# Moving the x loads, the bias additions and the key copies in the hand-written end of an attention stage

## The chip, the core and the metric

The kernel runs on one core of one Trainium2 chip. The metric is the device time in microseconds (us). Engines are named as in the profile: PE is TensorE, DVE is VectorE, ACT is ScalarE, POOL is GpSimd, SP is SyncE, which here only issues DMAs.

## The reference, cut to what matters

The computation has two layers, both with a residual. The first is cross-attention of 3200 tokens (32 batches of 100, 512 features) on a context of 722 rows, with a causal mask, so that only the first 100 context rows of a batch count. The second is a feed-forward layer with 16 routed experts and a shared one.

```python
def xattn(Q, K, V, WQ, WK, WV, Wfc, bfc):            # 16 heads of 32
    q, k, v = heads(Q @ WQ.T), heads(K @ WK.T), heads(V @ WV.T)
    scores = einsum('bhqd,bhkd->bhqk', q, k) / sqrt(32)
    attn = softmax(where(tril(ones(Sq, Skv)), scores, -inf))
    y = einsum('bhqk,bhkd->bhqd', attn, v)
    return y.transpose(0, 2, 1, 3).reshape(B, Sq, 512) @ Wfc.T + bfc

def ffn(h):
    # each expert takes its 12 best tokens of each batch by softmax(h @ gate_w.T):
    # cap = int(100 * 2.0 / 16)
    out = scatter_add((gelu(x_tok @ Wg[e].T) * (x_tok @ Wu[e].T)) @ Wd[e].T * topk_w)
    return out + (gelu(h @ Ws_g.T) * (h @ Ws_u.T)) @ Ws_d.T

x = x + xattn(layernorm(x), ctx, ctx, ...)
x = x + ffn(layernorm(x))
```

## The kernel before, in words

Every projection splits its float32 operands into a high and a low part and makes three matmul passes into one PSUM bank (`mm3`, L56).

**Units.** Attention is cut into 32 units u = 4 * sb + c: a super-block sb of four batches (400 tokens) and a chunk c of four heads. A unit consists of these steps, each a small function:

- `kload` (L210) loads the keys of the unit from DRAM into kt; `vload` (L215) loads the values v of a super-block.
- `qproj`/`qkeep`: q = normed x times WQ on PE into a "kv" PSUM buffer, copied to SBUF by ACT (L230).
- `scores`: 16 small matmuls into sc (L240).
- `sm_max` (DVE, L251, eight per half, two halves hb), `sm_sub` (POOL, L260), `sm_exp` (ACT, L264), `sm_sum` (DVE, L269 and L270), `sm_mul` (POOL, L275): the softmax.
- `turns`/`keeps` (`p_turn` on PE, L281; `p_keep` on ACT, L286): the probabilities transposed, one pair of batches at a time, and copied to pt.
- `values`: pt times v (L296). `y_keep`: split by ACT (L101) and DVE (L102), written to DRAM (yD, L306).

The keys and values themselves are projected on the way, block j and chunk ck at a time: `kproj` puts keys into a kv buffer, `kkeep` copies them to kk on ACT (L204) and writes them to kD on SP (L205); `vproj`/`vkeep` do the same for values in three of four iterations. In the iteration with ck = 3 (`vv` is false) there is no value projection.

**The loop.** The units run as a software pipeline. Iteration u (u from 0 to 28) projects q of unit u, does the softmax of unit u - 1, turns and values of unit u - 2, and y of unit u - 3. The kernel is under a manual schedule: every engine runs its instructions in the order in which the program states them, and SP issues its DMAs in that order into one queue. DMA completion uses eight semaphores in turn, so that each issue on SP also waits for the DMA eight before it. PSUM has two kv buffers and two ms buffers (turns, values).

**The end.** Units 29, 30 and 31 are written out by hand in `last_units`. Between their steps stand those of the feed-forward layer's first group of three 128-row tiles, the object `pr`. `pr.load_y` loads the attention output (yh, yl, L1003). For tile i, `pr.load_x(i)` loads x (L1011), `pr.bias(i)` adds bfc to it on POOL (L1014), `pr.fc(i)` is y times Wfc on PE into a kv buffer (L56), `pr.add(i)` adds the two on DVE (L1023), `pr.stats(i)` (DVE, L1029, L1030), `pr.rsqrt(i)` (POOL, L1036, L1037) and `pr.norm(i)` (DVE, L1044) are the layer norm, and `pr.turn(i)` transposes the tile on PE (L955), after which ACT and DVE make the parts xh and xl (L956, L957). `F.chunk_load` loads a chunk of expert weights (wraw, L705), `F.chunk_cast` and `F.chunk_low` split it on ACT (L713) and POOL. `F.begin` starts the feed-forward matmuls (gate-up "gu", then down "dn"), which fill the rest of the kernel.

The order around the change, in the code before:

```python
            u = NU - 3
            scores(u - 1)
            y_keep(u - 3)
            kload(u)
            vload(nsb - 1)
            for i in range(pr.nt):
                pr.load_x(i)
            F.chunk_load()
            kload(u + 1)
```

Of the kernel before, what the change touches and what calls it, by code (L numbers as in the profile page):

```python
# [60 lines left out]
def attention(tc, K, F):  # L61
    nc = tc.nc
    with ExitStack() as ctx, ExitStack() as kvctx:
# [34 lines left out]
        nsb = K.nsb  # L98
# [114 lines left out]
        def vload(sb):  # L213
            v = vp.tile([S, 4, D], F32, name="v")
            nc.sync.dma_start(v, K.vD[sb * SB:(sb + 1) * SB, :].rearrange("(b s) d -> s b d", b=4))  # L215
            for b in range(4):
                cur["v", sb, b] = v[:, b, :]
# [167 lines left out]
        def turns(u, *bs):  # L385
            for b in bs:
                p_turn(u, b)
# [12 lines left out]
        def last_units(pr):  # L400

            gp = nc.gpsimd

            def maxes(u):
                for hb in range(2):
                    sm_max(u, hb)
                    sm_sub(u, hb)

            u = NU - 3
            scores(u - 1)  # L410
            y_keep(u - 3)
            kload(u)
            vload(nsb - 1)
            for i in range(pr.nt):
                pr.load_x(i)
            F.chunk_load()
            kload(u + 1)
            maxes(u - 1)
            qkeep(u, qproj(u))
            turns(u - 2, 0, 1)  # L420
            keeps(u - 2, 0, 1)
            turns(u - 2, 2, 3)
            sm_exp(u - 1, 0)
            keeps(u - 2, 2, 3)
            sm_exp(u - 1, 1)
            for hb in range(2):
                sm_sum(u - 1, hb)
                sm_mul(u - 1, hb)
            pr.fc(0)
            values(u - 2)  # L430

            u = NU - 2
            scores(u - 1)
            y_keep(u - 3)
            F.chunk_load()
            pr.bias(0)
            pr.bias(1)
            maxes(u - 1)
            pr.add(0)
            pr.stats(0)  # L440
            pr.rsqrt(0)
            qkeep(u, qproj(u))
            turns(u - 2, 0, 1)
            sm_exp(u - 1, 0)
            keeps(u - 2, 0, 1)
            sm_exp(u - 1, 1)
            pr.fc(1)
            for hb in range(2):
                sm_sum(u - 1, hb)
                sm_mul(u - 1, hb)  # L450
            turns(u - 2, 2, 3)
            keeps(u - 2, 2, 3)
            F.chunk_cast(0, 0)
            pr.norm(0)
            pr.add(1)
            kload(u + 1)
            values(u - 2)

            u = NU - 1
            scores(u - 1)  # L460
            y_keep(u - 3)
            pr.store(0)
            pr.bias(2)
            pr.stats(1)
            maxes(u - 1)
            pr.rsqrt(1)
            pr.fc(2)
            qkeep(u, qproj(u))
            F.ask(1, lambda: ps_kv.tile([128, D], F32, name="kv"))
            F.preps[1].load_x(0)  # L470
            F.preps[1].load_x(1)
            turns(u - 2, 0, 1)
            sm_exp(u - 1, 0)
            keeps(u - 2, 0, 1)
            pr.add(2)
            sm_sum(u - 1, 0)
            sm_mul(u - 1, 0)
            sm_exp(u - 1, 1)
            pr.norm(1)
            turns(u - 2, 2, 3)  # L480
            keeps(u - 2, 2, 3)
            sm_sum(u - 1, 1)
            sm_mul(u - 1, 1)
            pr.stats(2)
            pr.turn(0)
            values(u - 2)
            pr.turn(1)
            F.chunk_cast(0, 1)
            pr.rsqrt(2)
            pr.store(1)  # L490

            scores(u)
            y_keep(u - 2)
            F.chunk_low(0, 0, gp)
            F.chunk_low(0, 1, gp)
            maxes(u)
            turns(u - 1, 0, 1)
            keeps(u - 1, 0, 1)
            turns(u - 1, 2, 3)
            keeps(u - 1, 2, 3)  # L500
            values(u - 1)
            F.preps[1].fc(0)
            pr.norm(2)
            sm_exp(u, 0)
            sm_sum(u, 0)
            sm_mul(u, 0)
            sm_exp(u, 1)
            pr.turn(2)
            y_keep(u - 1)
            sm_sum(u, 1)  # L510
            sm_mul(u, 1)
            pr.store(2)
            F.chunk_cast(0, 2)
            scctx.close()
            F.open_gu()
            F.begin(pr.done())
            F.chunk_low(0, 2, gp)
            F.preps[1].bias(0)
            F.preps[1].add(0)
            for i in range(3):  # L520
                F.chunk_cast(1, i)
                F.chunk_low(1, i, gp)
            F.preps[1].bias(1)
            turns(u, 0, 1)
            keeps(u, 0, 1)
            pr.logits()
            turns(u, 2, 3)
            keeps(u, 2, 3)
            F.begun()
            values(u)  # L530
            pr.tokens()
            y_keep(u)

        with tc.manual_schedule(engines={mybir.EngineType.Pool}):
            prologue()
            for u in range(NU - 3):
                sb, c = divmod(u, NC4)
                a, back = u - 1, u - 2
                a = a if a >= 0 else None
                back = back if back >= 0 else None  # L540
                j, ck = divmod(u - KS, NC4)
                j += 2
                kv = j in blocks
                vv = kv and ck < KVB[j]
                jn, d = divmod(u + NC4 - KS, NC4)
                jn += 2
                jl, dl = divmod(u + NC4 + 2 - KS, NC4)
                jl += 2
                xs = sb + 1 < nsb
                xn = divmod(u + 5, NC4) if u + 5 < NU else None  # L550
                if u > 0:
                    kload(u)
                if jl in blocks and (jl, dl) != (3, 0):
                    ctx_load(jl, dl)
                sn, bn = divmod(u + 6, NC4)
                if sn < nsb:
                    x_load(sn, bn)
                if FC_AT <= u < FC_AT + NC4:
                    fr = load_w(3, u - FC_AT)
                if u == FC_AT + NC4:  # L560
                    F.load_consts()
                if u == FC_AT + NC4 + 2:
                    F.split_consts()
                if a is not None:
                    scores(a)
                if u - 3 >= 0:
                    y_keep(u - 3)
                if a is not None:
                    sm_max(a, 0)
                    sm_sub(a, 0)  # L570
                    sm_max(a, 1)
                    sm_sub(a, 1)
                qkeep(u, qproj(u))
                if a is not None:
                    sm_exp(a, 0)
                if back is not None:
                    p_turn(back, 0)
                    p_turn(back, 1)
                    p_keep(back, 0)
                    p_keep(back, 1)  # L580
                if xn:
                    x_stats(*xn)
                if a is not None:
                    sm_exp(a, 1)
                    sm_sum(a, 0)
                    sm_mul(a, 0)
                if kv:
                    kkeep(j, ck, kproj(j, ck))
                if c == 1:
                    vload(sb)  # L590
                if back is not None:
                    p_turn(back, 2)
                    p_turn(back, 3)
                    p_keep(back, 2)
                    p_keep(back, 3)
                if a is not None:
                    sm_sum(a, 1)
                    sm_mul(a, 1)
                if xn:
                    x_norm(*xn)  # L600
                if jn in blocks:
                    ctx_split(jn, d)
                if FC_AT <= u < FC_AT + NC4:
                    F.fc_split(u - FC_AT, fr)
                if u == 0:
                    vkeep(1, 1, vproj(1, 1))
                if vv:
                    vkeep(j, ck, vproj(j, ck))
                if xs:
                    x_turn(sb + 1, c, vv)  # L610
                if back is not None:
                    values(back)
            kvctx.close()
            F.open_first()
            pr = F.prep(0, lambda: ps_kv.tile([128, D], F32, name="kv"),
                        lambda: ps_ms.tile([128, NC4, 128], F32, name="ms"))
            pr.load_y()
            last_units(pr)
# [690 lines left out]
```

## Time and profile before

| | us |
|---|---|
| three runs | 1692.14, 1692.4, 1695.08 |
| median | 1692.4 |
| the profiled execution: time | 1691.74 |
| its span in the profile | 1689.5 |
| PE busy | 1665.4 (99%) |
| DVE busy | 921.2 (55%) |
| ACT busy | 679.7 (40%) |
| POOL busy | 624.3 (37%) |

The span runs from the first to the last recorded instruction of the execution. "Busy" is the time in which an engine works on an instruction. The clock that PE is granted is a number between 0 and 1; its mean over this execution is 0.996. A wait is named by the engine that waits, the instruction that waits, and the one whose end released it, as `PE ms L281 <- ACT pt L286`. The profile's durations come from this one execution.

### The profile page before, as it was taken

Reading aid. Unit: us, or ns where it says so; the run is one execution under the profiler, and the core shown is the slowest. Engines: PE = TensorE matmul, PEld = TensorE weight load, DVE = VectorE, ACT = ScalarE, POOL = GpSimd, SP = SyncE. Lnnn points to the kernel's source line nnn. Section 1 sums busy time; section 2 is a strip of 40 time slices with the busy share of each in tenths; the row PEclk is TensorE's granted clock in tenths of the full one; section 3 lists DMA queues with packets and bytes.
Section 4 is the critical chain, followed back from the end, with each engine's and each line's share of the span. In section 5 each row is a group of like instructions: output and inputs, shape, how many; then the busy total and the mean of one; then the engine's idle time right before and its main releaser. Section 6 shows DMA issues by size and latency. Waiting matters only on the chain.

```text
span 1689.5 us, 28055 instructions
## 1 busy us (share of the span) xinstructions
PE 1665.4 (99%) x10854; PEld 1531.3 (91%) x10854; DVE 921.2 (55%) x2208; ACT 679.7 (40%) x1088; POOL 624.3 (37%) x541
## 2 busy tenths in 40 slices
PE   8999999989999999999999999999999999999999
PEld 7998889869989999989899999999999999999998
DVE  4878777655433434344555555555555555555542
ACT  4556555443111111122434444444444444444442
POOL 3877777570111011010243444333344333344011
PEclk9999999989999999999999999999999999999999
DMA  7555544545322214211445554555554455555452
GB/s 219 160 161 181 160 160 152 173 159 183 101 78 98 75 68 139 87 44 42 142 155 159 167 165 143 160 152 151 165 168 144 157 160 151 160 163 157 134 165 63
DMA packets 106741, 237.46 MB, mean 141 GB/s; under 512 B 13777, under 2 KB 58034, under 8 KB 106608
## 3 DMA queue, kind: packets, MB, share of 16 engines
q1 hardware_dynamic: 93248, 209.98, 37.4%
q0 software_dynamic: 12944, 25.22, 7.7%
q8 instruction: 85, 1.39, 0.3%
q10 hardware_dynamic: 416, 0.48, 0.1%
q14 instruction: 48, 0.39, 0.1%
HBM read 181.90 MB, written 53.73 MB: 139 GB/s over the span
## 4 chain that ended last, share of the span: by engine, by line
PE 93%; ACT 2%; DMA 2%; DVE 1%; POOL 1%; issue 1%; SPq 0%; ACTq 0%; POOLq 0%; DVEq 0%
PE gu L56 49%; PE dn L56 24%; PE kv L56 11%; PE m L56 3%; PE ms L281 2%; PE ms L296 2%; PE sc L240 1%; POOL p L260 1%; DMA x<-x 1%; ACT pt L286 1%; DMA kD<-kk 1%; PE m L1078 1%; DVE p L251 1%; PE ms L171 0%; ACT p L264 0%
## 5 line engine op out<-in xcount | busy, mean ns | idle before, releaser
L56 PE MATMUL gu<-xh,whl 128*128 128x384 f32 (+1 forms) x3200 | 643.8, 333 | 0.7 <-ACT xh L956 0.7
L56 PEld LDWEIGHTS gu<-xh,whl 128*128 128x128 f32 x3200 | 558.9, 188 | 17.8 <-ACT xh L956 0.9
L56 PE MATMUL dn<-whl,hh 128*128 128x512 f32 x1168 | 368.0, 396 | 0.0
L730 DVE TENSOR_TENSOR whl<-wraw,whl 128x1536 fp32r<-128x1536 f32 x142 | 249.7, 1758 | 205.7 <-ACT whl L729 205.6
L935 POOL DMA_INDIRECT gx<-xnD,iq x180 | 226.7, 1259 | 362.1 <-DVE big L966 301.9
L56 PE MATMUL gu<-xl,whl 128*128 128x384 f32 (+1 forms) x1600 | 337.2, 332 | 0.0
L56 PEld LDWEIGHTS gu<-xl,whl 128*128 128x128 f32 x1600 | 280.0, 188 | 0.1
L764 ACT CAST hh<-g 128x384 fp32r<-128x384 f32 (+1 forms) x200 | 100.9, 505 | 409.2 <-DVE g L761 409.2
L56 PEld LDWEIGHTS dn<-whl,hh 128*128 128x128 f32 x1168 | 215.8, 188 | 36.9
L761 DVE TENSOR_TENSOR g<-g,gu 128x384 f32<-128x384 f32 (+1 forms) x200 | 108.3, 541 | 247.9 <-PE gu L56 243.3
L729 ACT CAST whl<-wraw 128x1536 fp32r<-128x1536 f32 x142 | 209.7, 1477 | 64.8 <-PE dn L56 61.7
L56 PE MATMUL dn<-whl,hl 128*128 128x512 f32 x584 | 230.6, 395 | 0.0
L760 ACT ACTIVATE g<-gu 128x384 f32<-128x384 f32 (+1 forms) x200 | 96.3, 481 | 239.2 <-PE gu L56 239.1
L765 DVE TENSOR_TENSOR hl<-g,hh 128x384 fp32r<-128x384 f32 (+1 forms) x200 | 111.2, 556 | 114.2 <-ACT hh L764 114.2
L977 POOL DMA_INDIRECT out_dram<-x,isl x48 | 77.7, 1619 | 173.0 <-ACT x L976 163.2
L56 PEld LDWEIGHTS dn<-whl,hl 128*128 128x128 f32 x584 | 109.8, 188 | 26.2
L260 POOL TENSOR_TENSOR p<-p,mx 100x800 f32<-100x800 f32 x64 | 96.6, 1529 | 65.6 <-DVE mx L251 64.3
L275 POOL TENSOR_TENSOR p<-p,sm 100x800 f32<-100x800 f32 x64 | 101.1, 1583 | 9.6 <-DVE sm L270 6.1
L251 DVE CUSTOM_DVE_ANT_0 p<-sc,mask 100x100 f32<-100x100 f32 x512 | 95.3, 255 | 0.0
L1014 POOL TENSOR_TENSOR x<-x,bfc 128x512 f32<-128x512 f32 x23 | 30.2, 1332 | 163.9 <-DMA x<-x 128.0
L269 DVE TENSOR_REDUCE sm<-p 100x8 f32<-100x800 f32 x64 | 63.1, 986 | 27.1 <-ACT p L264 27.1
L967 ACT CAST xh<-big 128x512 fp32r<-128x512 f32 x59 | 36.7, 622 | 101.6 <-DVE big L966 101.6
(155 smaller groups left out, 1646.9 us busy)
## 6 DMA issues: line engine op xcount, KB each, us to landing
wraw<-wE SPq DMA_DIRECT2D x144, 768.0 KB
yD<-y SPq DMA_DIRECT2D x31, 400.0 KB
xt<-x SPq DMA_DIRECT2D x32, 200.0 KB
vD<-vt SPq DMA_DIRECT2D x25, 256.0 KB
kt<-kD SPq DMA_DIRECT2D x32, 200.0 KB
v<-vD SPq DMA_DIRECT2D x8, 800.0 KB
xnD<-xn SPq DMA_DIRECT2D x25, 256.0 KB
out_dram<-x SPq DMA_DIRECT2D x25, 256.0 KB
```

The source lines that it names most:

```text
L56: r = nc.tensor.matmul(out, t[0][a], t[1][b], start=(first and i == 0), stop=(last and i == n - 1))
L251: nc.vector.tensor_tensor_reduce(out=p[:, bb, h, :], in0=sc[:, h, cs], in1=mask, scale=ISCALE, scalar=NEG, op0=ALU.add, op1=ALU.max, accum ...
L260: nc.gpsimd.tensor_tensor(pv, pv, mx[:, :, None].to_broadcast([S, 8, S]), ALU.subtract)
L275: nc.gpsimd.tensor_tensor(pv, pv, sm[:, :, None].to_broadcast([S, 8, S]), ALU.mult)
L729: nc.scalar.copy(h, r)
L730: nc.vector.tensor_tensor(l, r, f32(h), ALU.subtract)
L760: nc.scalar.activation(g[:, 0:t], pg[:, 0:t], AF.Gelu)
L761: nc.vector.tensor_tensor(g[:, 0:t], g[:, 0:t], pu[:, 0:t], ALU.mult)
L764: nc.scalar.copy(hh[:, 0:t], g[:, 0:t])
L765: nc.vector.tensor_tensor(hl[:, 0:t], g[:, 0:t], f32(hh[:, 0:t]), ALU.subtract)
L935: nc.gpsimd.indirect_dma_start(out=g[:, k, :], out_offset=None, in_=self.K.xn.rearrange("t (a f) -> (t a) f", f=128), in_offset=bass.Indir ...
L977: ins = nc.gpsimd.indirect_dma_start(out=self.K.out, out_offset=bass.IndirectOffsetOnAxis(ap=r.isl[:, i:i + 1], axis=0), in_=o, in_offset= ...
```

## The change

It reorders instructions in two places and adds none.

In the loop, the ACT copy of the keys and its DMA (`kkeep`) go behind the two last copies of the probabilities (`p_keep(back, 2)` and `p_keep(back, 3)`) in iterations without a value projection.

In `last_units`, the three loads of x go ahead of the y write of unit 26, of the values' load and of the weight load, and the keys of unit 30 go ahead of values and weights; on POOL, `bias(1)` goes behind the two subtractions of unit 29; on PE, `fc(2)` goes from ahead of the q projection of unit 31 to behind it and behind the first turns of unit 29; on DVE, `add(2)` goes behind the two sums of unit 30, and the second sum of unit 31 goes ahead of the y split of unit 30.

```diff
@@ last_units
             u = NU - 3
             scores(u - 1)
-            y_keep(u - 3)
             kload(u)
-            vload(nsb - 1)
             for i in range(pr.nt):
                 pr.load_x(i)
+            y_keep(u - 3)
+            kload(u + 1)
+            vload(nsb - 1)
             F.chunk_load()
-            kload(u + 1)
             maxes(u - 1)
...
             F.chunk_load()
             pr.bias(0)
+            maxes(u - 1)
             pr.bias(1)
-            maxes(u - 1)
             pr.add(0)
...
             pr.rsqrt(1)
-            pr.fc(2)
             qkeep(u, qproj(u))
...
             turns(u - 2, 0, 1)
             sm_exp(u - 1, 0)
             keeps(u - 2, 0, 1)
-            pr.add(2)
+            sm_exp(u - 1, 1)
+            pr.fc(2)
             sm_sum(u - 1, 0)
             sm_mul(u - 1, 0)
-            sm_exp(u - 1, 1)
             pr.norm(1)
             turns(u - 2, 2, 3)
             keeps(u - 2, 2, 3)
             sm_sum(u - 1, 1)
             sm_mul(u - 1, 1)
+            pr.add(2)
             pr.stats(2)
...
             sm_exp(u, 1)
+            sm_sum(u, 1)
+            sm_mul(u, 1)
             pr.turn(2)
             y_keep(u - 1)
-            sm_sum(u, 1)
-            sm_mul(u, 1)
             pr.store(2)
@@ the loop
-                if kv:
-                    kkeep(j, ck, kproj(j, ck))
+                pk = kproj(j, ck) if kv else None
+                if kv and vv:
+                    kkeep(j, ck, pk)
...
                     p_keep(back, 2)
                     p_keep(back, 3)
+                if kv and not vv:
+                    kkeep(j, ck, pk)
```

## The prediction

> **What bounds the kernel now.** I read the page first: TensorE (PE) is busy for 99% of the span and carries 93% of the chain that ended last, so only time in which PE stands or runs at a lower clock can be won. The PE row and the clock row place that time: a slice is 42.2 us, and apart from the start only slice 9 (338 to 380 us) shows an 8, in both rows.
>
> ```profile
> PE   8999999989999999999999999999999999999999
> ...
> PEclk9999999989999999999999999999999999999999
> ...
> PE 93%; ACT 2%; DMA 2%; DVE 1%; POOL 1%; issue 1%; SPq 0%; ACTq 0%; POOLq 0%; DVEq 0%
> ```
>
> Next I read the chain of waits from 320 to 350 us (start, length, what). The chain goes through 11.63 us in which it waits for the first x tile, asked for at 326.65.
>
> ```profile
> 326.65 11.63 DMA x<-x
> 338.27 0.03 POOLq L1014
> ...
> 339.65 1.26 POOL x L1014
> 340.91 1.49 POOL p L260
> ...
> 343.20 0.48 ACT pt L286
> 343.69 0.14 issue
> 343.82 1.54 PE ms L281 x8
> 345.36 1.53 PE ms L296 x32
> ```
>
> Then the timeline of single engines (start, duration, engine, line, operation, in brackets the idle time before it and who ended it). GpSimd's two bias additions (L1014) stand ahead of its subtraction of the row maxima (L260), so the whole softmax of unit 29 waits for x. PE, which has three matmul passes of group 0's projection (L56, fc(1)) to do meanwhile, still stands for 4.05 us.
>
> ```profile
> 338.67 1.10 PE L56 MATMUL kv<-wfh,yl 128*128 128x512 f32 x4
> 343.82 1.54 PE L281 MATMUL ms<-ident,p 100*100 100x100 f32 x8 [4.05 <-ACT pt L286]
> ...
> 356.28 0.86 PE L281 MATMUL ms<-ident,p 100*100 100x100 f32 x8 [1.14 <-ACT pt L286]
> 357.74 0.75 PE L955 MATMUL ms<-ident,xn 128*128 128x128 f32 x4 [0.59 <-ACT pt L286]
> 358.42 0.89 PE L296 MATMUL ms<-pt,v 100*32 100x100 f32 x32
> 359.96 0.91 PE L955 MATMUL ms<-ident,xn 128*128 128x128 f32 x4 [0.65 <-DVE xl L957]
> ```
>
> Last, windows of 5 us (busy time and instructions of each engine, the granted clock, DMA share, GB/s): after the gap the clock is at a half.
>
> ```profile
> 340.00:345.00 5.00, 1.18 (x8) 1.21 (x8) 2.61 (x6) 2.57 (x5) 4.92 (x6) 0.83 0.71 285
> 345.00:350.00 5.00, 5.00 (x71) 3.94 (x70) 4.55 (x20) 1.78 (x4) 4.10 (x3) 0.50 0.22 81
> 360.00:365.00 5.00, 4.88 (x52) 3.80 (x52) 3.25 (x25) 2.83 (x6) 3.90 (x6) 0.66 0.21 77
> ```
>
> From 380 us on, PE is busy 50.00 of every 50 us. [...]
>
> **Part 1: key copies behind probabilities (`kkeep` after `p_keep`).** It acts in the seven iterations whose block has no value projection (u = 4, 8, ..., 28). There ACT copies kk (0.48 us) between the exponentials and the last two pt copies, and PE waits with values:
>
> ```profile
> 281.58 0.48 ACT L204 COPY kk<-kv 128x384 f32<-128x384 f32 x1
> 281.94 0.91 ACT L286 COPY pt<-ms 100x400 f32<-100x400 f32 x2
> ...
> 282.51 0.89 PE L296 MATMUL ms<-pt,v 100*32 100x100 f32 x32 [0.44 <-ACT pt L286]
> ```
>
> The seven waits are 0.41, 0.45, 0.43, 0.44, 0.41, 0.44 and 0.78 us. With the copy out of the way ACT starts pt about 0.37 us sooner, and the exponential before it ends at 281.69, so not all 0.44 can go. Nor is all kept: GpSimd's and DVE's chain of the next iteration isn't earlier, and its turns had only about 0.3 us of slack behind that chain. I take 0.3 for each of six (0.15 to 0.4): -1.8 (-1.0 to -2.4). For u = 28 I take 0.36 and count it in part 2. What the copy delays: kv has two buffers, so the next unit's q projection waits for it, with about 0.85 us of slack; and its kD write leaves about 0.8 us later. SP's queue is in order, so what follows waits with it: only at u = 28 does anything urgent follow, yh and yl, where yl lands at 331.0 by my reckoning and fc(0)'s third pass wants it at 330.6, up to 0.45, inside the range.
>
> **Part 2: the last three units.** I worked it through in order of time.
>
> x: the three loads no longer stand behind the write yD, v and their issue times. By the SP rows, kt(29) now goes at 325.1 and x at 325.6 to 327.5, 1.05 sooner. Queue order holds in the trace (yl landed at 330.2, v at 337.9, x at 338.3), so x also loses 1.2 MB ahead of it (yD 400 KB, v 800 KB). After yl, kt and x are 1.0 MB; at the 390 to 400 GB/s of 329 to 331 us that is 2.5 us: x0 at 332.2, x2 at 333.5. GpSimd is busy until 333.5 with the last multiplication of unit 28. x is off the path. On SP, yD(26) now goes behind x; its tile is one of two and is wanted again by y(28) after 341, while the write ends near 335, so nothing waits. kt(30) goes sooner, and kt(31)'s issue, which waited for v (337.93), now waits for x1.
>
> GpSimd: bias(0) 1.26 to 334.8, both subtractions of unit 29 (1.5 each) to 338.1, then bias(1), now behind them, to 339.4; only add(1) needs it, and that waits for fc(1) until 340.1 anyway, so this move costs nothing. ACT's exponentials of 0.87 each follow from 336.6 and 338.1.
>
> A new wait: fc(1)'s kv buffer is now the one of fc(0), so fc(1) waits for DVE's add(0), which stands behind sixteen maxima. They end at 336.5, and the addition takes 0.69: 337.25. fc(1) wants to start at 336.35, so 0.95 is lost (nothing, if PE is late anyway), and behind it in PE's order stand the second turns of unit 28. They end at 340.8 instead of 345.36.
>
> v: now behind x, yD and kt(30). What is moved ahead of it is 0.8 MB more x and kt(30), so its 0.82 MB begin near 335 where they began at 331. Its rate while it moves is 223 to 248 GB/s in the trace, together with its neighbours. The Trainium skill, "DMA: Bandwidth & Descriptors", section "Why a DMA increments its semaphore by 16 and not by 1", says that a transfer takes the largest divisor up to 16 of its outer dimension in engines, so v's 100 rows use ten; and its section "Queues, rings and completion order" has each engine take its share in order. That speaks against this change, for a ten-engine transfer now waits behind 16-engine ones. By the row (0.82 MB at 235 GB/s, 0.7 from last byte to landing) v lands at 339.3; by the rule, with wraw1's and yD's shares mixed in, at 342.5. I take 341.1: values(28) then starts at 341.2, not 345.33. By the rule alone, 342.6, 1.4 us of the gain gone.
>
> Next late: wraw1, now behind v, and ACT's cast of it (L713). The cast ran at 345.85 and could run at 341.3; I put its landing at 342.9 (341 to 344). Behind the cast in ACT's order are y(28) and, through DVE's maxima and GpSimd's subtraction, unit 30's exponentials, so this comes back ahead of the second turns of unit 29, 1.05 at most, for fc(2) now stands between (2.8 us at full clock) and covers the 1.14 that stood there. fc(2) itself costs nothing: it is moved on PE, not added.
>
> Clock: the gap of 4.05 was followed by 6.8 us at half clock (343.3 to 350.2). PE was busy for 6.4 of them with work that takes 3.2 at full clock, so 3.2 were lost. With no gap above 1.1 us there, this goes; it is inside the 5.4 below.
>
> The DVE order costs something: add(2), 0.7 us, is now between sum(30,1) and stats(2), ahead of xl(0), for which turn(1) waits: 0.65 before becomes about 1.9. Sum for this point: turn(0) at 351.3, values(29) at 351.8, turn(1) at 354.55 instead of 359.96: -5.4. From there the same chain runs.
>
> The second drop in clock (360.4 to 363.8, up to 1.7 us lost): the Trainium skill, "TensorE: Matmul & The Clock Gate", Part 1, says that the clock halves after an idle window of about 3.4 us, and Part 4 that transposes do not count as busy in the same way. The row agrees with a window (0.66 above) though no gap before it exceeds 1.14 us, among turns and values. By Part 1 read alone the drop would go with the gaps; by Part 4 it stays, for the turns stay and the wait at turn(1) is longer. I keep it: 0, or -1.7 if it goes.
>
> Sum of part 2: gate-up starts at 364.8 instead of 370.29, -5.5; with wraw1 a little sooner, -6.1. I take -5.6 to -5.8 (-3 to -8.5), u = 28's 0.36 included. The feed-forward stage behind it is PE-bound and keeps its length.
>
> **Sum.** -5.7 - 1.8 = -7.5. The profiled execution took 1691.74 (span 1689.5 and 2.2 around it), so about 1684.3; it lies 0.66 under the median of 1692.4, so 1685.0 for a median.
>
> **Rivals and chances.** About 0.2%, 3.4 us, is what a measurement of this kernel can tell from no change; faster is under 1689.0, slower over 1695.8.
>
> Forecast, 0.55: -5 to -9.5.
>
> B, 0.27: x's wait is passed to v and wraw1. If v lands at 343.5 or later and the cast follows, PE gets another gap near the old one and perhaps one half-clock window; gain 3 to 5, near 1688.5. For it: DMA engines 100% busy from 329 to 340. Against: the queue drains at over 400 GB/s once v is through.
>
> C, 0.13: v and wraw1 come in time and the second drop goes too: -5.7 - 1.8 - 1.7, and about 1.9 that I charge to the waits of the cast and of turn(1), make -11: near 1681.5.
>
> D, slower, 0.05: the added dependence of fc(1) on add(0). It decides only if x0 lands after about 340, beyond the old 338.3: then fc(1)'s 2.98 us no longer fill the gap but come behind bias and maxima, twice as long at half clock, 5.96; less what the sooner subtractions save, +3 to +5: near 1696. Queue order speaks against.
>
> That the change does not do what it says is excluded: these engines run in program order, and x's three issues stand ahead of yD and v in SP's.
>
> The range, 1680.5 to 1689.5, takes in the forecast's bounds, most of B and half of C. Faster 0.86 (forecast, C, and 0.18 of B), same 0.09 (the rest of B), slower 0.05 (D).
>
> **What would show it.** x lands at 332 to 334 and GpSimd has no wait for it; PE's 4.05 gap is gone and the clock is 1.00 from 340 to 350; PE waits about 1 us for DVE ahead of fc(1); values(28) waits on v; ACT's first cast waits for wraw; turn(1) waits about 2 us for xl; the six waits of 0.4 at L296 are near 0.1; gate-up starts near 363. Wrong: x later than 338, a gap of 3 us before values(28), or gate-up at 368 or later.

## The result, and the profile after

The changed kernel took 1689.64 us in the median of 15 runs (1686.01 to 1691.85), the kernel before 1693.75 in 15 runs beside it (1692.14 to 1695.08): ratio 0.9977, 95% interval 0.997 to 0.9984. A second series later gave 0.9982 (0.9976 to 0.9989). So the change gains 3 to 4 us, about half of the 7.4 forecast, and the measured median lies 0.14 us above the top of the range. The forecast counted from a median of 1692.4; the median measured beside the change is 1.35 us higher, so the 0.14 says little. What is wrong is the size of the gain.

The two profiled executions can't be subtracted from end to end. In the changed kernel's, the first values (L296) start at 60.61 us, in the one before at 58.75, in code that the change does not touch: the granted clock is at a half for about 6.8 us of the start in one and for 3.4 in the other, and a piece of 3.4 us of half clock costs up to 1.7. That is not all of it: with one piece at the start, four profiles have the first values at 58.75 to 60.13. Below, values(n) is the values step of unit n, and "relative" times count from the first values. The feed-forward stage behind the first gate-up matmul is the same, 1319.2 us in both. What the change does is seen in when gate-up starts: relative 309.08 after (369.69 - 60.61), 311.54 before. The profiled gain is 2.5 us.

x is off the path. GpSimd's first bias addition waited for the x load before the change and starts without a wait after it (before, then changed):

```profile
338.40 2.52 POOL L1014 TENSOR_TENSOR x<-x,bfc 128x512 f32<-128x512 f32 x2 [4.57 <-DMA x<-x]
335.15 1.29 POOL L1017 TENSOR_TENSOR x<-x,bfc 128x512 f32<-128x512 f32 x1
```

PE's waits in the last units (total, times, longest), changed kernel:

```profile
PE ms L958 <- DVE xl L960: 2.9, 1, 2.9
PE ms L296 <- ACT pt L286: 1.1, 3, 0.4
PE kv L56 <- DVE x L1026: 0.8, 1, 0.8
```

The wait of 4.0 for ACT's pt is gone. The new wait for add(0) (L1026) is 0.77; the prediction had 0.95, though its own figures (337.25 less 336.35) give 0.90. But turn(1), which waited 0.65 for xl(0), now waits 2.9. PE's timeline of the changed kernel (L958 is turn):

```profile
338.99 1.19 PE L56 MATMUL kv<-wfh,yh 128*128 128x512 f32 x4 [0.77 <-DVE x L1026]
...
343.02 1.01 PE L296 MATMUL ms<-pt,v 100*32 100x100 f32 x32 [0.30 <-ACT pt L286]
...
352.14 0.75 PE L958 MATMUL ms<-ident,xn 128*128 128x128 f32 x4 [0.59 <-ACT pt L286]
352.82 0.89 PE L296 MATMUL ms<-pt,v 100*32 100x100 f32 x32
356.63 0.75 PE L958 MATMUL ms<-ident,xn 128*128 128x128 f32 x4 [2.92 <-DVE xl L960]
```

Relative to the first values, values(28) is 4.2 us sooner than before (282.41 against 286.58), turn(0) 7.5, turn(1) still 5.2, but gate-up only 2.5. The last loss is in the clock. Windows of 5 us of the changed kernel:

```profile
340.00:345.00 5.00, 4.70 (x82) 3.69 (x81) 4.70 (x7) 3.01 (x6) 4.92 (x6) 1.00 0.87 308
345.00:350.00 5.00, 5.00 (x30) 4.54 (x31) 4.01 (x35) 1.21 (x2) 3.90 (x4) 1.00 0.55 204
...
355.00:360.00 5.00, 3.23 (x43) 2.74 (x44) 3.25 (x13) 1.65 (x4) 4.42 (x5) 0.76 0.31 117
360.00:365.00 5.00, 5.00 (x47) 3.73 (x46) 4.12 (x31) 3.35 (x6) 3.23 (x3) 0.50 0.24 85
365.00:370.00 5.00, 4.32 (x16) 3.40 (x15) 1.52 (x3) 1.16 (x4) 3.00 (x2) 0.71 0.00 0
```

The first half-clock stretch (343 to 350 before) is gone, as forecast; the second, 3.4 us before, is now 10.2 us long (357.6 to 367.9). From turn(1) to gate-up it takes 13.06 us (356.63 to 369.69) where it took 10.33. The longer wait ahead of turn(1) does not by itself make this stretch longer: the run x_fc2 below has the same wait of 2.92, and with 3.4 us of half clock it takes 10.27 there.

So the changed kernel has as much half clock in these units as before, only later. That is no accident of one profile: the mean clock over the whole span is on average 0.9960 in 126 runs of the kernel before and 0.9959 in 36 of the changed one. A piece of 3.4 us takes 0.001 off it.

Why xl(0) is late is seen on DVE and POOL: first norm(1) before the change, then DVE and POOL in the changed kernel.

```profile
356.93 0.50 DVE L1044 TENSOR_SCALAR xn<-x,mv,rs 128x512 f32<-128x512 f32 x1
```

```profile
351.61 1.76 DVE L1047 TENSOR_SCALAR xn<-x,mv,rs 128x512 f32<-128x512 f32 x1 [0.19 <-POOL rs L1040]
353.29 0.97 DVE L269 TENSOR_REDUCE sm<-p 100x8 f32<-100x800 f32 x1
354.30 0.20 DVE L270 RECIPROCAL sm<-sm 100x8 f32<-100x8 f32 x1
354.42 0.64 DVE L1026 TENSOR_TENSOR x<-kv,x 128x512 f32<-128x512 f32 x1
355.09 0.70 DVE L1032 BATCH_NORM_STATS2 bst<-x 128x6 f32<-128x512 f32 x1
...
355.92 0.66 DVE L960 TENSOR_TENSOR xl<-ms,xh 128x512 fp32r<-128x512 f32 x1
```

```profile
351.01 0.57 POOL L1040 TENSOR_TENSOR rs<-rs,nhalf 128x1 f32<-128x1 f32 x1
351.56 1.52 POOL L275 TENSOR_TENSOR p<-p,sm 100x800 f32<-100x800 f32 x1
```

norm(1) (L1047), 0.50 us before, takes 1.76: POOL's multiplication of unit 30 started 0.05 us ahead of it, ends at 353.08, and norm(1) ends 0.29 behind that. The Trainium skill, "SBUF — State Buffer", section "SBUF: two separate sides", says that DVE and GpSimd share a pair of ports as an exclusive lock, for a DVE instruction in a two-port mode or with two inputs in SBUF: whichever starts first has it for its whole instruction, and the other stands still. These rows fit it; that norm(1) runs in a two-port mode is not shown by any run here.

### The profile page after: what moved, and what is told of

Its sections match the earlier page's. It is cut to its first block, busy times and chain, and to the rows that moved or that the text cites. A ratio compares the mean times of both kernels' runs of the same rounds, so it can differ in the third digit from the quotient of the medians.

```text
span 1688.8 us, 28043 instructions
## 1 busy us (share of the span) xinstructions
PE 1668.2 (99%) x10854; PEld 1532.8 (91%) x10854; DVE 923.6 (55%) x2208; ACT 679.8 (40%) x1088; POOL 625.1 (37%) x541
## 4 chain that ended last, share of the span: by engine, by line
PE 94%; DVE 2%; ACT 1%; POOL 1%; issue 1%; DMA 1%; ACTq 0%; POOLq 0%; DVEq 0%
PE gu L56 49%; PE dn L56 24%; PE kv L56 11%; PE m L56 3%; PE ms L281 2%; PE ms L296 2%; POOL p L260 1%; PE sc L240 1%; DVE p L251 1%; ACT pt L286 1%; PE m L1081 1%; PE ms L171 0%; DMA kD<-kk 0%; PE m L958 0%; DVE y L102 0%
```

## The experiments

Each kernel had 5 to 21 runs beside the kernel before. The ratio is over all runs; the other columns are of one profiled execution each. "Half clock" is worked out from 1-us windows of the last units as the sum of 2 x (1 - clock).

| kernel | ratio to before, 95% | values(25) / values(28) / gate-up, relative | wait at turn(1) | norm(0), norm(1) | half clock |
|---|---|---|---|---|---|
| before | 1 | 255.9 / 286.6 / 311.5 | 0.65 | 0.50, 0.50 | 10.2 |
| changed | 0.9977 (0.997-0.9984) | 255.8 / 282.4 / 309.1 | 2.92 | 1.81, 1.76 | 10.2 |
| after_again | 0.9982 (0.9976-0.9989) | 255.7 / 282.3 / 308.3 | 2.92 | 1.81, 1.76 | 10.2 |
| kk_only | 1.0004 (0.9996-1.0012) | 255.8 / 287.7 / 310.5 | 0.17 | 0.50, 0.50 | 6.8 |
| kk_cx | 0.999 (0.9982-0.9998) | 254.1 / 287.1 / 309.6 | 0.65 | 0.50, 0.50 | 6.8 |
| end_only | 0.9987 (0.998-0.9993) | 255.9 / 282.0 / 311.0 | 1.87 | 3.20, 1.75 | 17.1 |
| x_back | 1.0018 (1.0011-1.0024) | 255.7 / 287.8 / 312.8 | 2.92 | 3.20, 1.76 | 10.2 |
| x_only | 0.996 (0.9946-0.9974) | 255.9 / 282.0 / 305.4 | none | 0.49, 0.50 | 6.8 |
| x_bias | 0.9973 (0.9962-0.9984) | 255.9 / 282.0 / 307.3 | 1.46 | 3.20, 1.75 | 6.8 |
| x_fc2 | 0.9978 (0.997-0.9987) | 255.9 / 282.0 / 305.8 | 2.92 | 0.50, 1.76 | 3.4 |
| x_kk | 0.9965 (0.9951-0.9979) | 255.8 / 282.4 / 304.8 | 0.65 | 0.50, 0.50 | 0 |
| x_cx | 0.9953 (0.9939-0.9966) | 254.0 / 280.6 / 303.6 | 0.66 | 0.50, 0.49 | 3.4 |
| norm_late | 0.9974 (0.9965-0.9984) | 255.8 / 282.4 / 305.5 | 1.83 | 1.81, 0.50 | 3.4 |
| xl_first | 0.9967 (0.9955-0.9979) | 255.7 / 282.3 / 304.5 | 1.40 | 1.81, 1.75 | 0 |
| both | 0.9956 (0.9942-0.9969) | 255.8 / 282.5 / 303.6 | 0.58 | 1.81, 0.50 | 0 |
| fill | 0.9977 (0.9967-0.9988) | 255.9 / 282.6 / 305.2 | none | 1.81, 0.49 | 6.8 |
| both_cx | 0.9948 (0.9934-0.9961) | 254.0 / 280.6 / 301.7 | 0.58 | 1.81, 0.50 | 0 |
| both_cx_add | 0.9953 (0.9939-0.9966) | 254.1 / 279.9 / 302.0 | 0.58 | 1.78, 0.50 | 0 |
| no_block | 0.9945 (0.9932-0.9959) | 254.0 / 280.8 / 303.2 | 0.58 | 0.49, 0.50 | 3.4 |
| no_block_add | 0.995 (0.9937-0.9964) | 254.0 / 279.9 / 301.8 | 0.58 | 0.50, 0.50 | 0 |

A profiled execution can be far from its kernel's median: that of x_fc2 is the fastest of 12 runs (1686.91 against 1689.55), that of end_only the slowest of 20 (1693.2 against 1691.38). So gate-up and half clock compare two kernels only roughly.

**The loop part alone (kk_only), and why it gains nothing.** Only the loop's hunk on the kernel before:

```diff
-                if kv:
-                    kkeep(j, ck, kproj(j, ck))
+                pk = kproj(j, ck) if kv else None
+                if kv and vv:
+                    kkeep(j, ck, pk)
...
+                if kv and not vv:
+                    kkeep(j, ck, pk)
```

> The kernel before with the loop part alone (kkeep behind p_keep). Theory: the 0.38 us that values gains in each of seven iterations is given back in the next one, at the second turns, which wait for ACT's copy of the first turns and thereby for the exponential, whose chain (ACT y, DVE y and maxima, GpSimd subtraction) is as long as before. So the values of units 2, 6, 10 start without the 0.4 us wait and those of units 3, 7, 11 as late as before: net -0.3 to 0 us, ratio 0.9998 to 1.0. Rival, the prediction's part 1: -0.3 us kept each time, -1.8 to -2.2 us, ratio 0.9987.

Ratio 1.0004: nothing. Values(2) starts 0.37 us sooner (relative 18.78 against 19.15), values(3) no sooner (29.85 against 29.89). The give-back is seen in PE's timeline (values(14), the second turns of the next iteration), two lines before the change and two of the changed kernel:

```profile
201.28 0.89 PE L296 MATMUL ms<-pt,v 100*32 100x100 f32 x32 [0.44 <-ACT pt L286]
...
208.08 0.85 PE L281 MATMUL ms<-ident,p 100*100 100x100 f32 x8
```

```profile
202.69 0.89 PE L296 MATMUL ms<-pt,v 100*32 100x100 f32 x32
...
209.77 0.94 PE L281 MATMUL ms<-ident,p 100*100 100x100 f32 x8
```

The second turns start 6.80 us after values(14) before the change and 7.08 after it, and the next values come 11.07 us after these, where it was 10.70. The turns wait for ACT's copy of the first ones, that for the exponential, and that for the subtraction and the maxima behind the y split; and ACT's y cast at 204.07 comes 1.38 us after the start of values(14), where it was 1.00 (202.28), because kk, cxh (L135, the copy of the next context chunk) and xnh (L101, the high part of the next normed x) still stand ahead of it.

kk_only also shows that the loop part changes which kv buffer fc(1) gets: with x late it waits 3.75 us for add(0), and values(28) is 1.1 us later than before.

**The copy that holds y (kk_cx).** On kk_only, in the same iterations, cxh (`ctx_split`) goes behind the y split of the following iteration:

```diff
-                if jn in blocks:
+                late = (jn, d) if jn in blocks and kv and not vv else None
+                if jn in blocks and not late:
                     ctx_split(jn, d)
...
                 if u - 3 >= 0:
                     y_keep(u - 3)
+                if late:
+                    ctx_split(*late)
+                    late = None
```

> The kernel before with the loop part, and in the same seven iterations the copy of the next context chunk on ACT (cxh, L135, 0.4 us) put behind the y split of the following iteration. Theory of the give-back: what takes the 0.38 us back is ACT's chain pt, kk, cxh, xnh, y, of unchanged length, ahead of DVE's y and maxima. With cxh out of it y comes 0.4 sooner, so 0.3 us is kept in each iteration: the values of units 3, 7, 11 start 10.7 us after those of unit 2, 6, 10 instead of 11.05, and the values of unit 25 start 253.9 us after the first instead of 255.8. Rival, it is another wait (the kv buffer, GpSimd's sequence): the values of unit 25 stay at 255.8. The time: -1.5 to -2 against the loop part alone, which measured 1.0004.

Values(3) comes at 29.51, values(25) at 254.06: 1.7 us are kept over six iterations. The explanation of the give-back stands: some 0.3 us an iteration were to be had, but only with cxh out of the y cast's way too. The late cxh without the loop part was not run, so what each of the two gives by itself is open.

**The last units without the loop part (end_only), and with x late (x_back).** end_only is the changed kernel with the loop's hunk undone; x_back has SP's order of before:

```diff
+            y_keep(u - 3)
             kload(u)
+            vload(nsb - 1)
             for i in range(pr.nt):
                 pr.load_x(i)
-            y_keep(u - 3)
-            kload(u + 1)
-            vload(nsb - 1)
             F.chunk_load()
+            kload(u + 1)
```

> The changed kernel with the loop part undone. Theory: all of the gain is in the last units: -3.5 to -4.5 us against the kernel before, ratio 0.9975 to 0.998, the same as the whole change. Rival (the loop part carries 1.8): -2 to -2.5 us, ratio 0.9987.

> The changed kernel with the order on SP as before (x behind the y write, the values and the keys), everything else of the change kept. The prediction's case D: fc(1) now waits for add(0), which waits for x; x lands at about 338.5 in the time of before, so fc(1) starts behind bias(0) and the maxima, at 340 to 341, the wait ahead of it is 3 us or more, and the values of unit 28 start 286 to 288 us after the first ones (282.4 in the changed kernel). Ratio to before 0.999 to 1.002. Rival, the order on GpSimd and PE carries the gain and x is early enough: ratio 0.9977 as the whole change.

end_only measured 0.9987, a smaller gain than the whole change's, though the intervals overlap. My theory that the last units carry all of it, unaltered, missed. Its profile, the slowest of its runs, has norm(0) at 3.20 and 17.1 us of half clock.

x_back measured 1.0018, 3 us slower than before, as case D of the prediction has it. PE's waits there:

```profile
PE kv L56 <- DVE x L1026: 3.9, 1, 3.9
PE ms L958 <- DVE xl L960: 2.9, 1, 2.9
```

fc(1) waits for x by way of add(0), then runs partly at half clock, and values(28) comes at 287.8. The new order on SP is worth 0.4% inside this change (0.9977 or 0.9982 against 1.0018), 6 to 7 us.

**The SP order alone, and one part more at a time.** x_only is the kernel before with the SP order of the change and nothing else (the keys of unit 30, the y write, the values and the weights move with x). x_bias adds bias(1) behind the subtractions; x_fc2 adds instead the moves of fc(2), add(2) and the sums; x_kk adds the loop part; x_cx that and the late cxh.

> The kernel before with the new order on SP alone (x and the keys of unit 30 ahead of the y write, the values and the weights). GpSimd still adds both biases (2.5 us) ahead of the subtractions, but from 333.9 and not from 338.4, so the exponentials and the values of unit 28 come up to 2 us after those of the whole change (values 284 to 285 after the first, before 286.6, changed 282.4), and PE's gap of 4.05 goes to 1 or less. Theory (x is the main term): ratio 0.997 to 0.9985. Rival (the order on GpSimd and PE is needed too): 0.9995 to 1.0005.

> The kernel with the new SP order alone, plus bias(1) behind the subtractions of unit 29 on GpSimd. Theory of the port: bias(1) now delays GpSimd's rsqrt(0) by 1.26 us, so that DVE's norm(0) comes free just as GpSimd goes from rsqrt(0) straight into the two multiplications of unit 29, and takes 1.8 to 3.2 us instead of 0.49; y(28), stats(1) and the maxima of unit 30 behind it on DVE come 1 to 2.7 us later. So this part of the change costs time: 1 to 3 us slower than the SP order alone (0.996), ratio 0.9968 to 0.998. Rival, the prediction's view: the softmax of unit 29 starts 1.26 sooner and the move costs nothing: 0.9953 to 0.996.

> The kernel with the new SP order alone, plus the change's moves of fc(2) on PE and of add(2) and the sums on DVE; bias(1) stays. Theory of the port and of DVE's order: norm(0) stays at 0.5 us, since GpSimd's order is that of before; norm(1) may be blocked (1.7 us) and add(2) stands ahead of xl(0), so turn(1) waits 1.5 to 2.9 us where the SP order alone shows no wait: 0.5 to 3 us slower than that (0.996), ratio 0.9965 to 0.998. Rival, the prediction's view: fc(2) covers the gap of 1.14 ahead of the second turns and this part gains 1: 0.995.

> The kernel with the new SP order alone, plus the loop part (kkeep behind p_keep). In the loop alone it was worth nothing (1.0004), but the kv buffers come out in another order with it, and fc(1) waits for add(0): 0.7 us with early x. Theory: ratio 0.9955 to 0.9965, within 1 us of the SP order alone, with a wait of 0.7 to 0.8 ahead of fc(1). Rival, the loop part gains in a kernel whose last units no longer wait for x: 0.995 or less.

> As the kernel before it in this list, with the late context copy in the loop (1.7 us sooner at the values of unit 25). If the last units keep it, this is the fastest so far: ratio 0.9945 to 0.995, -8.5 to -9.5 us. Rival, the gain is lost again to half clock in the last units: 0.996.

x_only measured 0.996, against 0.9982 for the whole change in the same series, and the intervals do not overlap: one hunk gives more than all of them. (With the first series' 0.9977 they overlap a little, from 0.997 to 0.9974.) The mean clock of its five runs is 0.9978 where the changed kernel has 0.9959. Values(28) is as early as in the whole change, so bias(1) ahead of the subtractions costs nothing there; that expectation of mine (up to 2 us later) was wrong. The other parts of the change each gave a higher ratio than x_only, though with intervals that overlap it. x_kk, at 0.9965, is the closest, with a wait of 0.75 us ahead of fc(1), as expected. x_cx measured 0.9953, a little short of what was expected, with values(25) 1.9 us sooner than in x_only and gate-up 1.8. The traces show what x_bias and x_fc2 do. DVE's norm(0) in x_only and in x_bias:

```profile
342.82 0.49 DVE L1044 TENSOR_SCALAR xn<-x,mv,rs 128x512 f32<-128x512 f32 x1
```

```profile
341.95 3.20 DVE L1044 TENSOR_SCALAR xn<-x,mv,rs 128x512 f32<-128x512 f32 x1
```

and POOL in x_bias:

```profile
341.33 0.57 POOL L1037 TENSOR_TENSOR rs<-rs,nhalf 128x1 f32<-128x1 f32 x1
341.86 3.00 POOL L275 TENSOR_TENSOR p<-p,sm 100x800 f32<-100x800 f32 x2
```

With bias(1) between, POOL's rsqrt(0) ends just when DVE is ready for norm(0), and the multiplications start 0.09 us ahead of it. In x_only DVE's sums of unit 29 come later, so norm(0) comes free 1.3 us after the first multiplication has started (341.50 to 343.02): it takes 0.49, and the second multiplication takes 1.65 instead of 1.52. That it misses the long wait there is a matter of when DVE gets to it. In x_bias the maxima and exponentials of unit 30 come later behind it, and the second turns of unit 29 wait 2.00 us instead of 1.14. In x_fc2 norm(0) is 0.50, but norm(1) 1.76 and the wait at turn(1) 2.92: this part of the change brings that wait with it.

**Two moves on DVE (norm_late, xl_first, both).** On the changed kernel:

```diff
-            pr.norm(1)
             turns(u - 2, 2, 3)
             keeps(u - 2, 2, 3)
             sm_sum(u - 1, 1)
+            pr.norm(1)
             sm_mul(u - 1, 1)
-            pr.add(2)
-            pr.stats(2)
             pr.turn(0)
+            pr.add(2)
+            pr.stats(2)
```

norm_late has the move of norm(1), xl_first that of add(2) and stats(2), both has the two.

> The changed kernel, with DVE's norm(1) moved behind the second sum of unit 30, and nothing else. Theory, a blocked port: norm(1) took 1.76 us instead of 0.50 because GpSimd's multiplication of unit 30 ran from 351.56 to 353.08 at the same time. Behind the sum it starts when that is over and takes 0.5 to 0.6; xl(0) and turn(1) come 1.0 to 1.3 us sooner, PE's wait at turn(1) falls from 2.9 to about 1.7, and the time by 1.2 to 3 (more if a window of half clock goes with it): ratio to before 0.996 to 0.997. Rival, the length is the instruction's own after its wait for rsqrt(1): it stays at 1.7 us and so does the wait of 2.9; ratio 0.9977 as the whole change.

> The changed kernel, with DVE's xl(0) of turn(0) ahead of add(2) and stats(2), and nothing else. Theory, the order on DVE: xl(0) comes 1.5 us sooner (0.64 + 0.70 + 0.18), PE's wait at turn(1) falls from 2.9 to about 1.4 us, the gate-up matmuls start 1.5 us sooner or more, and the half clock behind it gets shorter or stays: -1.5 to -4 against the whole change, ratio to before 0.9955 to 0.997. Rival, another chain (exponential and sums of unit 30) ends at the same time: turn(1) waits as long, ratio 0.9977.

> The changed kernel with both DVE moves: norm(1) behind the second sum of unit 30, and xl(0) of turn(0) ahead of add(2) and stats(2). If the blocked port and the order on DVE are two separate terms of the wait of 2.9 us at turn(1), they add up: the wait is 0.5 to 0.8, and gate-up starts 304 us after the first values or sooner (309.1 in the changed kernel, 305.5 and 304.5 with one move each). Ratio to before 0.995 to 0.9965, and no half clock in the last units in most executions. Rival, one hides the other: as the order alone, 0.9967.

norm(1) behind the sum, from norm_late:

```profile
352.61 0.50 DVE L1047 TENSOR_SCALAR xn<-x,mv,rs 128x512 f32<-128x512 f32 x1
```

So the 1.76 was not the instruction's own. In time norm_late gains nothing that can be told from the changed kernel (0.9974 against 0.9977 and 0.9982), where 0.996 to 0.997 was expected; the mean clock of its ten runs is 0.9960, no higher either. The waits at turn(1) are 2.92, 1.83, 1.40 and 0.58: the two terms take off 1.1 and 1.5, together 2.3. In xl_first turn(1) comes 1.3 us sooner, relative, than in the changed kernel (294.68 against 296.02), but gate-up 4.6 sooner: no half clock is left, and turn(1) to gate-up takes 9.82 us instead of 13.06. Its PE line and its windows:

```profile
355.54 0.75 PE L958 MATMUL ms<-ident,xn 128*128 128x128 f32 x4 [1.40 <-DVE xl L960]
```

```profile
355.00:360.00 5.00, 3.56 (x52) 2.73 (x52) 4.71 (x25) 2.84 (x6) 4.33 (x5) 1.00 0.55 197
360.00:365.00 5.00, 4.69 (x51) 3.49 (x49) 3.87 (x20) 2.65 (x5) 4.36 (x4) 1.00 0.11 38
```

"both" gains what was forecast for the change, 7.4 us (0.9956), with 1.2 us between its fastest and slowest of five runs, where the changed kernel's 15 spread over 5.8. The mean clock of these five is 0.9988.

**Matmuls in the gap (fill).** On "both", `F.preps[1].fc(0)` goes from behind `values(u - 1)` to ahead of `pr.turn(1)`.

> As the kernel with both DVE moves, and on PE the matmuls of group 1's first tile (2.98 us, fc(g1,0)) ahead of turn(1) instead of behind the values of unit 30. Theory of the clock: what lowers it is a stretch of some 3 us in which PE does little but wait and transpose; with matmuls put into that stretch no half clock is left in any execution, and the wait at turn(1) is 0: the same work, gate-up 0.5 to 1 us sooner, and the spread over runs falls to that of the start. Ratio to before 0.994 to 0.996. Rival, the clock follows the transposes themselves wherever they stand: half clock comes back at turns(30), 3.4 us or more, no gain over both.

It missed: 0.9977. The wait moved. turn(2), which the matmuls had covered, now waits for norm(2), gate-up waits for xh, and the half clock stands at gate-up:

```profile
363.74 0.72 PE L958 MATMUL ms<-ident,xn 128*128 128x128 f32 x4 [0.74 <-DVE xn L1047]
366.40 1.65 PE L56 MATMUL gu<-xh,whl 128*128 128x384 f32 x4 [1.94 <-ACT xh L959]
```

**The second profile (after_again).**

> The changed kernel once more, for a second profile. Theory of the clock: half clock in the last units comes in pieces of 3.4 us whose number changes from execution to execution (three in the first profile); ahead of the wait at turn(1) everything repeats within 0.3 us: wait at turn(1) 2.9, fc(1) 0.77, values of unit 28 at 282.4, and gate-up differs from the first profile's 309.08 only by 1.7 us for each piece more or less. Rival: the pieces are a fixed consequence of the order of work: three again.

Three pieces again, though shifted (354.5 to 364.7), so the rival is not excluded. The theory missed in one point: with as many pieces gate-up was at 308.31, 0.8 sooner.

**Everything together.** both_cx is "both" with the late cxh; both_cx_add has add(0) between the two groups of maxima of unit 29; no_block and no_block_add are the same two with bias(1) again ahead of the subtractions.

> Both DVE moves of the last units on the changed kernel, and the late context copy in the loop. If the two are independent their gains add: 7.3 us of the one and 1.7 of the other, less what u = 28 already has: -8.5 to -9.5 against the kernel before, ratio 0.9945 to 0.995, gate-up 301.8 us after the first values (303.56 without the late copy). Rival: the last units, which hang on DVE and GpSimd, give the 1.7 us back as the loop did with the first 0.38: 0.9956.

> As the kernel before it in this list, with add(0) on DVE between the two groups of eight maxima of unit 29, so that fc(1) finds its kv buffer free. Theory: the wait of 0.75 us ahead of fc(1) goes, the values of unit 28 start 0.5 us sooner and so does gate-up; the second subtraction of unit 29 is 0.4 us later, with slack. Ratio 0.994 to 0.9947. Rival: the later exponential is the next thing that is late, and nothing is gained: as without it.

> The kernel with both DVE moves and the late context copy (0.9948), with bias(1) on GpSimd again ahead of the subtractions of unit 29, as before the change. Theory of the port: that was the second blocked place, norm(0) at 1.81 us; it falls to 0.5, the maxima of unit 30 and what follows come 0.5 to 1.3 us sooner, and the values of unit 28 are no later (281.97 and 282.00 in the two orders measured without the rest). Gate-up 300.5 to 301.3 us after the first values (301.72), ratio 0.9935 to 0.9945. Rival, the later exponential of unit 29 takes it back: 301.7 or more, 0.9948 or more.

> As the kernel before it in this list, with add(0) on DVE between the two groups of maxima of unit 29. fc(1) no longer waits 0.76 us, and the values of unit 28 are the next to be late, for v (0.49 us in the kernel that had this move with bias(1) late). Expected: gate-up within 0.5 us of the kernel before it, ratio 0.993 to 0.9945. Rival: the second exponential of unit 29 comes 0.7 later behind it, and the second turns wait: 0.5 to 1 us slower than without the move.

The loop's gain and the last units' add up (0.9948 for both_cx, gate-up at 301.7). Freeing norm(0) as well took it from 1.81 to 0.49 but brought gate-up no sooner, as the rival said; no_block's values(29) are at 290.51, both_cx's at 290.42. Without the wait of fc(1), values(28) waits for v instead, 0.49 and 0.62 us, and no gain in time shows (0.9953 and 0.995, both short of what was expected). The lowest ratio, 0.9945 (1683.74 us), can't be told from the other three.

## Why the prediction was wrong

**Right.** x is off the path and the order on SP is the main term. The 4.05 gap and the half clock behind it went. fc(1)'s new wait was 0.77 (0.95). The second turns' gap of 1.14 is covered. From the values of unit 25 on, turn(1) came 5.1 us sooner (relative 5.19 less the loop's 0.13); the prediction's working had 5.4. Case D was a true mechanism: x_back showed it, and with bias(0), the first to need x, only 0.5 us later than before (relative 280.18 against 279.65), where the prediction wanted x0 beyond 340.

**Wrong, part 1 (-1.8).** "Its turns had only about 0.3 us of slack": the six waits ahead of values went as forecast (none is above 0.15 us), but the loop gave only 0.13 us to the values of unit 25. Around 208 us before the change, PE's second turns started 0.16 us after the first copy that frees their buffers (207.92) and 0.11 after the second (208.31); in the changed kernel it is 0.05 after either. So there was a slack of about 0.1 us, and the chain through ACT's y had not got shorter.

**Wrong, the clock ("I keep it: 0, or -1.7 if it goes").** This is the step that failed most. The prediction took the half clock behind the old gap as gone and the second drop as staying or going. The second drop could also grow, and did, from 3.4 to 10.2 us: turn(1) to gate-up took 13.06 and 12.33 us in two executions, 10.33 before and 9.82 at full clock. That is 2.0 to 2.7 lost against the forecast, which let "the same chain" run. I bounded this term on one side only. With part 1's 1.7 that is 3.7 to 4.4 us, and 3.3 to 4.4 of the 7.4 are missing. Over all runs, too, the clock that was to rise by about 0.002 with the old gap's 6.8 us did not (0.9960 before, 0.9959 after); with the SP order alone it did (0.9978).

**Wrong in composition.** The wait at turn(1), put at about 1.9, was 2.92. add(2) and stats(2) ahead of xl(0) cost 1.5 and the blocked norm(1) 1.1; the prediction counted only add(2)'s 0.7, since stats(2) stood there before, and had no term for norm(1). turn(0) came about 1 us sooner than worked out, so that the sum at turn(1) came out nearly right is luck; the half clock begins within 1.2 us of turn(1) in both profiles (1.0 behind it in one, 1.1 ahead of it in the other). Neither v nor wraw1 kept anyone waiting in the changed kernel, so case B was wrong, and the rule on ten engines cost nothing that shows; v ended a wait only when add(0) was moved up.

**Open.** How many half-clock pieces an execution gets. With x early, waits at turn(1) of 0.6 to 1.5 went with 0, 3.4 or 6.8 us, 1.83 with 3.4, 1.87 with 17.1, 2.92 with 3.4 or 10.2, and no wait at all with 6.8. One program differs from run to run: x_kk's five runs have mean clocks of 0.999, 0.994, 0.994, 0.999 and 0.998. That fewer pieces explain the narrow spread of "both" is not shown: both_cx and x_kk, whose profiles have no half clock in these units either, spread over 3.0 and 3.9 us in five runs.

## What to carry to other kernels

Ahead of a reordering, follow the freed wait two waits further, and read a slack off the very instruction that would wait. On DVE a duration is not a constant: norm took 0.50, 1.76 or 3.20 us here, by what GpSimd had started just before; look which of the two starts first. Read the clock of every run and not of one profile alone. Try each hunk alone: here one of them was faster than all of them.

## What was not expected of the hardware

A DVE instruction of 0.50 us took 1.75 to 1.81 us when a GpSimd multiplication had started 0.04 to 0.08 us ahead of it. When two multiplications stood back to back it went both ways. In x_bias, end_only and x_back DVE didn't get in between the two and took 3.20 (x_bias: 3.00 for the pair). In the changed kernel norm(0) did, after 1.81, and POOL's pair took 3.27. What decides is open.

Half clock came after waits well below 3 us: in x_only the longest wait of PE in the ten microseconds ahead of its drop at 352.24 was 1.14 us.

```profile
348.93 0.85 PE L281 MATMUL ms<-ident,p 100*100 100x100 f32 x8
350.92 0.86 PE L281 MATMUL ms<-ident,p 100*100 100x100 f32 x8 [1.14 <-ACT pt L286]
352.38 1.13 PE L955 MATMUL ms<-ident,xn 128*128 128x128 f32 x4 [0.59 <-ACT pt L286]
```

The Trainium skill's rule of an idle window of about 3.4 us ("TensorE: Matmul & The Clock Gate", Part 1) would not have called that gap a danger. By Part 4, that transposes do not count as busy in the same way, it may be one: from 348.93 to the drop PE did nothing but turn and wait, for 3.3 us. But x_kk has the same turns with waits of 1.13 and 0.59 in its profile and no half clock, so no run here shows that this is the rule.
